# Graph layers on one core: the order of folds and first messages around a convolution

## The chip, the cores and the metric

The program runs on one core of one Trainium2 chip. The metric is the device time of one execution in microseconds (us), lower is better. TensorE multiplies matrices into PSUM, VectorE (DVE), ScalarE (ACT) and GpSimd (POOL) work elementwise, SyncE (SP) issues most transfers.

## The reference

Four graph layers follow each other on a tensor x of 8 batches, 2048 nodes and 64 features, each with a layer norm, a relu and a residual. The change lies in the second one (layer 1), a Chebyshev convolution with weights of its own for each node, and at the border to the third (layer 2), which takes three steps of messages over the same adjacency matrix:

```python
def _L1_gnn_ref(x, A, embedding, weight, bias):
    w = jnp.einsum('nd,dkio->nkio', embedding, weight)
    b = jnp.einsum('nd,do->no', embedding, bias)
    As = [jnp.eye(N, dtype=x.dtype), A, 2.0 * (A @ A) - I]
    x_g = jnp.einsum('knm,bmc->bnkc', jnp.stack(As, 0), x)
    return jnp.einsum('bnki,nkio->bno', x_g, w) + b
...
for _ in range(MAX_STEPS):        # layer 2, v = normed x
    effects = jnp.einsum('nm,bmd->bnd', adj_matrix, v)
    h = jax.nn.relu(jnp.einsum('bnk,dk->bnd', concat([v, effects]), W1) + b1)
    v = jnp.einsum('bnk,dk->bnd', h, W2) + b2
```

(The second listing is shortened; As stands for what the loop of the reference builds with K = 3.)

## The kernel before

Features lie on partitions, two batches in one tile of 128, so the 8 batches are four pairs (q = 0 to 3). The 2048 nodes are worked on in four chunks of 512 columns.

The stage concerned is the second half of `chebyshev_layer` (from L1338). `adj_product` (L302) forms adj times adj h for one chunk at a time. Its 16 steps m each load 128x512 of adj transposed (L313, five buffers), cast it on ACT into one of two buffers (L325), and issue eight matmuls of 512 columns: four with the high halves and four with the low halves of the stationary operand, into the PSUM banks pp0 to pp3. After each step it calls `after`, here `some` (L1359), which takes one piece of work off the list `waiting`. At the chunk's end it calls `done2` (L1364).

`done2` first empties the list. Then it loads 2 MB of node embeddings in two halves (emb, L1377) and the chunk of x (L1387), copies the product out of PSUM (L1389), and runs the convolution: for each pair q four blocks, each of four results `pk` of two products each (sixteen matmuls in the trace), which DVE multiplies by emb (L1416) and GpSimd then adds into two sums `acc` (L1421), four additions of a block, two in the first one. When a pair is done, a *fold* is put at the head of the list: `fold_up` (L1353) multiplies the two sums by `fold` into the bank `po` and adds the result to x (L1357). During the pair that follows, `some` takes it off at the block with `blk == 2`. The fold of the last pair stays on the list, and behind it come two pieces: `first` (L1430: the store of x and the first half of the next layer norm, with means by `center`, squares, sums by `to_rows`, root and reciprocal L273) and the second half (scale rows by `from_rows`, and the products into v, L1348). In the first three chunks these three are taken off after steps 0, 1 and 2 of the next chunk's product.

In the fourth chunk the list starts with twelve *first messages* (`first_messages`, one for each 128 nodes of the finished chunks): four small products of 128 columns, eight matmuls in the trace, from v into a bank `pk`, then a high half on ACT (L232) and a low half on DVE (L233). Here `some` is called at every block. Three of the 16 calls take a fold, twelve a message and the last finds nothing; the fold of the last pair, `first`, the second half and the four messages of the last chunk then follow in this order (L1437 to L1441) before layer 2. Layer 2 starts with a small matmul of `aa` and `wt`, and then its own `adj_product`.

The banks `pk` of the convolution, the messages and the norm rotate over three buffers of one name. Each engine works its instructions off in the order in which the build lays them down; a scheduler decides it, largely in the order of the source, and may take a ready piece ahead, as one `center` matmul before the last fold.

Of the kernel before, what the change touches and what calls it, by code (L numbers as in the profile page):

```python
# [27 lines left out]
NC = N // CW  # L28
# [99 lines left out]
class Kernel:  # L128
# [1144 lines left out]
    def chebyshev_layer(self, slots, k):  # L1273
# [29 lines left out]
        fold = k.tile([P, D], F, name="fold")  # L1303
# [34 lines left out]
        with (  # L1338
            tc.tile_pool(reuse_waits="tile", name="conv", bufs=2) as w,
            tc.tile_pool(reuse_waits="tile", name="conv_ps", bufs=1, space=PSUM) as ps,  # L1340
        ):
            steps, u_n = self.steps, self.source
            emb_dram = a["embT"]
            v = Halves(slots, "v", ("q0", "q1"), False)
            waiting = []

            def write(q, ch, xr, scale):
                nc.vector.tensor_mul(v(q)[:, ch * CW : (ch + 1) * CW], xr, scale)  # L1348

            def bank():  # L1350
                return ps.tile([P, CW], F, name="bank", tag="pk", bufs=3)

            def fold_up(x, q, accs):  # L1353
                po = ps.tile([P, CW], F, name="po")
                for i, h in enumerate((lo, hi)):
                    self.mm(po[h], fold, accs[i])
                nc.vector.tensor_add(x[:, q], po, x[:, q])  # L1357

            def some(*_):  # L1359

                if waiting:
                    waiting.pop(0)()

            def done2(ch, out):  # L1364
                while waiting:
                    some()
                if ch == 0:
                    steps.prepare(bank)
                if ch == NC - 1:
                    for t in range(NT - TC):  # L1370
                        waiting.append(
                            lambda t=t: steps.first_messages(v, u_n, t, bank())
                        )
                s = slice(ch * CW, (ch + 1) * CW)
                emb = slots.tile([P, NBLK, CW], F, name="emb", tag="q4")
                for j in range(2):
                    nc.sync.dma_start(  # L1377
                        emb[j * D : (j + 1) * D],
                        bass.AP(
                            tensor=emb_dram.tensor,  # L1380
                            offset=emb_dram.offset + j * N + ch * CW,
                            ap=[[0, D], [2 * N, NBLK], [1, CW]],
                        ),
                    )
                two = slots.tile([P, 2, NP, CW], F, name="two", tag="q5")
                aah, x = two[:, 0], two[:, 1]
                nc.sync.dma_start(x, self.xs[1][ch])  # L1387
                for q in range(NP):
                    nc.scalar.copy(aah[:, q], out[q])  # L1389
                free = 0  # L1390
                for q in range(NP):
                    accs = [w.tile([P, CW], F, name="acc", bufs=4) for _ in range(2)]
                    sides = list(enumerate(((xe, lo), (xo, hi))))
                    for blk in range(0, NBLK, 2):
                        pks = {}
                        for b in (blk, blk + 1):
                            for half, (src, h) in sides:

                                tag = ("pk", "pp0", "pp1", "pk", "pp2", "pp3", "pk")[free % 7]
                                free += 1  # L1400
                                pk = ps.tile(
                                    [P, CW], F, name="pk", tag=tag, bufs=3 if tag == "pk" else 1
                                )
                                pks[b, half] = pk
                                c = slice(b * P, (b + 1) * P)
                                self.mm(pk, w01[half][:, c], src(q)[:, s], stop=False)

                        for b in (blk, blk + 1):
                            for half, (src, h) in sides:
                                c = slice(b * P, (b + 1) * P)  # L1410
                                self.mm(pks[b, half], w2[h, c], aah[h, q], start=False)
                        for b in (blk, blk + 1):
                            for half in range(2):
                                acc = accs[half]
                                y = acc if b == 0 else w.tile([P, CW], F, name="y", bufs=3)
                                nc.vector.scalar_tensor_tensor(  # L1416
                                    y, pks[b, half], bias[:, b : b + 1], emb[:, b],
                                    op0=OP.add, op1=OP.mult,
                                )
                                if b > 0:  # L1420
                                    nc.gpsimd.tensor_add(acc, acc, y)  # L1421
                        if blk == 2:
                            some()
                        elif ch == NC - 1:
                            some()
                    waiting.insert(0, lambda q=q, accs=accs: fold_up(x, q, accs))
                std = w.tile([P, CW], F, name="std", tag="y", bufs=3)
                norm = self.norm_parts(ch, x, emb[:, :NP], aah, std, bank, write)

                def first():  # L1430
                    self.store_x(1, ch, x)
                    next(norm)

                waiting.extend((first, lambda: next(norm, None)))

            self.adj_product(ah_n, w, ps, done2, after=some, bufs=5, step=1, casts=2)
            while waiting:  # L1437
                some()

            for t in range(NT - TC, NT):  # L1440
                steps.first_messages(v, u_n, t, bank())  # L1441
# [922 lines left out]
```

## Time and profile before

| | us |
|---|---|
| median of three runs | 2153.69 |
| lowest and highest | 2149.0, 2154.99 |
| the profiled execution | 2148.51 |
| its span | 2146.8 |

Busy time over the span: PE (TensorE matmul) 1914.5 us (89%), DVE 1134.1 (53%), ACT 714.7 (33%), POOL 702.4 (33%). The four chunks of layer 1's convolution stage take the stretch from about 807 to 1350 us. A view of waits names the instruction that waited, the instruction that released it, the total, the number and the longest. A timeline shows start, length, engine, line, operation and tiles, the number of merged instructions, and in brackets the idle time before them and what ended it. A table of stretches gives for each engine the busy time and the number of instructions, then the share of TensorE's clock that was granted (1.00 is full), the share of the 16 DMA engines and what they moved.

### The profile page before, as it was taken

To read this page: it belongs to the slowest core of one execution; us is meant where nothing else is said; L and a number is where in the kernel's file an instruction comes from. 1 tells how busy PE (TensorE), PEld (TensorE's weight loads), DVE (VectorE), ACT (ScalarE), POOL (GpSimd) and SP (SyncE) were. 2 spreads that over 40 slices of the span, in tenths; PEclk is the share of its full clock that TensorE was granted. 3 is DMA by queue.
4 is the path that set the end of the run, shared out by engine and by line. 5 is a ranking of instruction groups with operands and counts; after the bars stand their busy time and mean duration, and the time that the engine had idled before them with its cause. 6 is when DMAs were issued, how large, how long until landed. Compare 5 with 4: busy or idle time off the path is not lost. (4 is left out here: it accounts for less than half of the span.)

```text
span 2146.8 us, 21291 instructions
## 1 busy us (share of the span) xinstructions
PE 1914.5 (89%) x7461; PEld 1153.1 (54%) x7466; DVE 1134.1 (53%) x1932; ACT 714.7 (33%) x1351; POOL 702.4 (33%) x595
## 2 busy tenths in 40 slices
PE   5868999977779999999999998999999999679875
PEld 1425766642237774353443543677777666345432
DVE  7877677737660224424334255698603222249774
ACT  6412555535543440020100201335335333258400
POOL 0000466765300006617357065001000000177770
PEclk8868999988869999999999999999999999879997
DMA  8230333441034360140320401456533443475665
GB/s 320 82 110 4 102 104 118 133 171 43 36 94 134 119 177 14 32 125 0 102 56 5 118 1 60 138 186 235 166 118 125 151 145 131 158 210 162 180 181 180
DMA packets 108797, 253.66 MB, mean 118 GB/s; under 512 B 20912, under 2 KB 21056, under 8 KB 101376
## 3 DMA queue, kind: packets, MB, share of 16 engines
q1 hardware_dynamic: 89264, 181.45, 26.7%
q0 software_dynamic: 17104, 66.47, 10.0%
q10 hardware_dynamic: 2304, 4.20, 0.5%
q8 instruction: 63, 1.03, 0.2%
q14 instruction: 62, 0.51, 0.1%
HBM read 218.30 MB, written 33.78 MB: 117 GB/s over the span
## 5 line engine op out<-in xcount | busy, mean ns | idle before, releaser
L325 ACT CAST adj<-adj_t 128x512 fp32r<-128x512 f32 x384 | 237.3, 619 | 685.9 <-PE pp L166 349.5
L1421 POOL TENSOR_TENSOR acc<-acc,y 128x512 f32<-128x512 f32 x224 | 277.1, 1268 | 444.9 <-DVE y L1416 444.9
L166 PE MATMUL pp<-adj,hi 128*128 128x512 f32 x1280 | 364.4, 404 | 4.4 <-ACT adj L325 4.2
L166 PE MATMUL pk<-q,w 128*128 128x512 f32 (+1 forms) x1024 | 356.5, 609 | 1.8 <-ACT q L1389 1.6
L166 PE MATMUL pp<-adj,lo 128*128 128x512 f32 x1280 | 356.3, 398 | 0.0
L166 PEld LDWEIGHTS pp<-adj,hi 128*128 128x128 f32 x1280 | 241.2, 190 | 77.0 <-issue 16.2
L166 PEld LDWEIGHTS pp<-adj,lo 128*128 128x128 f32 x1280 | 242.7, 190 | 55.6
L166 PEld LDWEIGHTS pk<-q,w 128*128 128x128 f32 (+1 forms) x1024 | 136.2, 188 | 210.2 <-issue 165.9
L1416 DVE SCALAR_TENSOR_TENSOR y<-pk,bias,q 128x512 f32<-128x512 f32 x224 | 157.7, 745 | 142.7 <-PE pk L166 133.2
L166 PE MATMUL acc<-q,ident 128*128 128x512 f32 x416 | 203.4, 615 | 28.4 <-DVE q L2151 16.4
L2061 POOL DMA_INDIRECT ring<-f_rows,near x121 | 140.3, 1160 | 67.5 <-issue 30.2
L166 PEld LDWEIGHTS acc<-q,ident 128*128 128x128 f32 x416 | 76.7, 195 | 104.7 <-issue 47.7
L2165 POOL IOTA q<- 128x2048 int32 x1 | 1.8, 1834 | 316.6 <-PE p L166 316.6
L166 PE MATMUL pp<-adj,x_ind_hi 128*128 128x512 f32 x256 | 94.7, 487 | 2.1 <-DVE q L751 1.9
L166 PE MATMUL bank<-std,from_rows 32*128 32x512 f32 x128 | 45.5, 858 | 54.4 <-DVE std L273 34.5
L1853 POOL TENSOR_TENSOR q<-q,beta 128x512 f32<-128x512 f32 x57 | 67.9, 1192 | 54.6 <-DVE beta L1829 30.8
L1416 DVE SCALAR_TENSOR_TENSOR acc<-pk,bias,q 128x512 f32<-128x512 f32 x32 | 22.6, 746 | 118.1 <-PE pk L166 118.1
L2132 DVE TENSOR_TENSOR q<-ring,e 128x1024 f32<-128x1024 f32 x58 | 70.0, 1218 | 9.3 <-PE acc L166 9.1
L273 DVE RECIPROCAL std<-std 128x512 f32<-128x512 f32 x16 | 53.6, 3351 | 36.7 <-ACT std L272 36.6
L166 PE MATMUL pp<-adj,x_ind_lo 128*128 128x512 f32 x256 | 71.7, 399 | 0.0
L1543 POOL DMA_INDIRECT q<-in_adj_dram,order x15 | 17.2, 1146 | 160.3 <-DVE top L1557 134.0
L166 PEld LDWEIGHTS pp<-adj,x_ind_hi 128*128 128x128 f32 x256 | 48.5, 190 | 38.7 <-issue 23.7
(410 smaller groups left out, 2695.8 us busy)
## 6 DMA issues: line engine op xcount, KB each, us to landing
adj_t<-in_adjT_dram SPq DMA_DIRECT2D x128, 512.0 KB, 3.9
adj_t<-in_adjT_dram SPq DMA_DIRECT2D x128, 256.0 KB, 3.3
rows<-in_adj_dram SPq DMA_DIRECT2D x16, 1024.0 KB, 6.0
q<-x SPq DMA_DIRECT2D x10, 1024.0 KB, 4.8
x<-q SPq DMA_DIRECT2D x9, 1024.0 KB, 4.0
q<-in_embT_dram SPq DMA_DIRECT2D x8, 1024.0 KB, 12.1
x_ch<-in_xT_dram SPq DMA_DIRECT2D x4, 1024.0 KB, 6.0
h_rows<-q SPq DMA_DIRECT2D x16, 256.0 KB, 3.6
```

What stands on the lines that cost most here:

```text
L166: self.nc.tensor.matmul(out, lhsT, rhs, start=start, stop=stop)
L273: nc.vector.reciprocal(std, std)
L325: nc.scalar.copy(moving, at[:, i])
L1416: nc.vector.scalar_tensor_tensor(y, pks[b, half], bias[:, b : b + 1], emb[:, b], op0=OP.add, op1=OP.mult,)
L1421: nc.gpsimd.tensor_add(acc, acc, y)
L1543: nc.gpsimd.indirect_dma_start(row, None, self.a["adj"], bass.IndirectOffsetOnAxis(ap=order[:, 1, t : t + 1], axis=0),)
L1853: self.nc.gpsimd.tensor_tensor(x, x, by.unsqueeze(2).to_broadcast([P, NB, D]), op=OP.mult)
L2061: self.nc.gpsimd.indirect_dma_start(to, None, self.kern.f_rows[:], bass.IndirectOffsetOnAxis(ap=index, axis=0))
L2132: nc.vector.tensor_tensor(y.rearrange("n i (b f) -> n i b f", b=NB), block[:, i : i + 2, : NB * D].rearrange("n i (b f) -> n i b f", b=NB) ...
L2165: nc.gpsimd.iota(whole, pattern=[[1, N]], base=0, channel_multiplier=0)
```

## The change

In the first three chunks an empty piece of work is put at the head of the list, so that step 0 of the next product is followed by nothing, step 1 by the fold, step 2 by `first` and step 3 by the second half. In the fourth chunk `some` is called only while more than five pieces are on the list, so that five messages (those of node tiles 7 to 11) are left; after the chunk these five, the last fold and the two halves of the norm are put into one hand-written order.

```diff
+            LEFT = 5
...
-                        if blk == 2:
-                            some()
-                        elif ch == NC - 1:
+                        if len(waiting) > LEFT if ch == NC - 1 else blk == 2:
                             some()
...
-                waiting.extend((first, lambda: next(norm, None)))
+                rest = first, lambda: next(norm, None)
+                if ch < NC - 1:
+
+                    waiting.insert(0, lambda: None)
+                    waiting.extend(rest)
+                else:
+                    fold, *left = waiting
+                    assert len(left) == LEFT
+                    waiting[:] = left[0], fold, left[1], rest[0], *left[2:], rest[1]
```

What a message is:

```python
pn = bank.rearrange("n (q f) -> n q f", q=NP)
for q in range(NP):
    self.kern.mm(pn[:, q], v(q)[:, t * P : (t + 1) * P], self.w1e)
self.kern.split(u_n, t, bank)
```

As built, the fourth chunk's end reads on TensorE: last convolution block, message 7, fold, message 8, four means, sums, messages 9 to 11, scale rows, messages 12 to 15. The line numbers of the changed kernel are one higher from L1344 on and seven higher behind this function.

## The prediction

> **What bounds the kernel now.** I read the table of stretches first, then TensorE's waits between 870 and 1345 us (the convolution stage of layer 1), then the timelines at the places where those waits lie. Stretches; the columns are length, busy time and instructions of PE, PEld, DVE, ACT, POOL, then TensorE's clock, DMA share and GB/s:
>
> ```profile
> 946.00:1037.90 91.90, 91.90 (x270) 34.47 (x268) 44.02 (x64) 2.88 (x6) 64.29 (x52) 1.00 0.02 7
> 1219.90:1322.70 102.80, 102.61 (x365) 45.19 (x363) 51.74 (x79) 8.59 (x16) 64.68 (x54) 1.00 0.00 1
> ```
>
> These are the convolutions of the second and the fourth chunk. TensorE is busy throughout, so what is moved about inside costs its own TensorE time and no more: the fourth holds twelve first messages, and (102.80-91.90)/12 = 0.91 us is the price of one. GpSimd is free a third of the time. So time is lost only where TensorE waits:
>
> ```profile
> PE po L166 <- POOL acc L1421: 8.2, 4, 2.8
> PE bank L166 <- DVE std L273: 4.2, 1, 4.2
> PE pp L166 <- ACT adj L325: 4.2, 3, 2.4
> PE pk L166 <- ACT q L1389: 1.6, 1, 1.6
> ```
>
> Some 20 us in all. The 8.2 us are four waits of the last fold of a chunk; the first three look alike:
>
> ```profile
> 899.40 1.27 PE L166 MATMUL pp<-adj,hi 128*128 128x512 f32 x4
> 900.51 1.09 PE L166 MATMUL pp<-adj,lo 128*128 128x512 f32 x4
> 903.40 2.29 PE L166 MATMUL po<-acc,fold 128*64 128x512 f32 x4 [1.80 <-POOL acc L1421]
> 905.63 1.19 PE L166 MATMUL pp<-adj,hi 128*128 128x512 f32 x4
> ```
>
> The first step of adj's product ends at about 901.6; the fold waits until 903.40 for GpSimd's last sums, and the second step stands behind it. The wait of 1.6 us, after the third chunk's product, is ACT's:
>
> ```profile
> 1083.62 0.62 ACT L325 CAST adj<-adj_t 128x512 fp32r<-128x512 f32 x1 [4.29 <-DMA adj_t<-in_adjT_dram]
> 1084.15 2.04 ACT L1389 COPY q<-pp 128x512 f32<-128x512 f32 x4
> ```
>
> ACT's queue holds the next chunk's first cast ahead of the four copies that the convolution needs, and that cast waits for a load that stands behind 1 MB of emb. Last, the end of the fourth chunk, and the clock (column after POOL) in it:
>
> ```profile
> 1322.76 1.13 PE L166 MATMUL bank<-q,center 128*128 128x512 f32 x2
> 1326.67 2.29 PE L166 MATMUL po<-acc,fold 128*64 128x512 f32 x4 [2.78 <-POOL acc L1421]
> 1328.89 2.84 PE L166 MATMUL bank<-q,center 128*128 128x512 f32 x6
> 1331.66 1.86 PE L166 MATMUL bank<-q,to_rows 128*32 128x512 f32 x8
> 1337.75 2.08 PE L166 MATMUL bank<-std,from_rows 32*128 32x512 f32 x6 [4.22 <-DVE std L273]
> 1342.60 5.36 PE L166 MATMUL bank<-w1e,q 128*128 128x128 f32 x32
> 1349.47 0.38 PE L166 MATMUL bank<-aa,wt 64*128 64x2 f32 x2 [1.51 <-DVE lo L233]
> ```
>
> ```profile
> 1323.00:1327.00 4.00, 1.22 (x3) 0.25 (x3) 2.42 (x4) 0.60 (x1) 4.00 (x4) 1.00 0.00 0
> 1338.00:1341.00 3.00, 2.23 (x7) 0.66 (x8) 1.89 (x8) 0.00 (x0) 0.00 (x0) 0.50 0.75 289
> 1344.00:1347.00 3.00, 3.00 (x21) 3.00 (x20) 1.82 (x9) 1.17 (x2) 0.29 (x1) 0.69 0.00 0
> ```
>
> From the last convolution matmul (1322.76) to layer 2's first (1349.47) are 26.7 us with little work: it waits for GpSimd, for the reciprocal, and then runs at half clock.
>
> **What the Trainium skill says.** "TensorE: Matmul & The Clock Gate", Part 1, What's actually happening: after about 3.4 us without work the TensorE clock halves, and about 3.4 us of work restore it. The trace agrees: after the wait of 2.78 us the clock stays 1.00, after the 4.22 us it is 0.50. "DMA: Bandwidth & Descriptors", Queues, rings and completion order: what one issuing queue puts on a DMA engine is consumed in order. That fits adj loads stuck behind emb: an emb half issued at 921.62, an adj load at 922.50, and the cast that needs it begins at 934.50.
>
> **The change part by part.** Counts of instructions on all engines stay; only their order changes (GpSimd's not at all).
>
> *1. Three chunk changes.* Built, the order becomes step 0, step 1, fold, step 2, mean and variance, then two steps and three matmuls more before the scale rows: everything of the old chunk comes one step later against adj. A step takes 1.83 us (lo matmuls start at 1198.85 and 1200.69). Step 1 can run at once: its cast, like step 0's, is done during the convolution (ACT is idle for 93 us before the cast of step 2 at 901.68). It ends at 903.4, just when the fold begins today; step 2 then stands where step 1 stood (905.63). Gain 1.80 each, 3 x 1.80 = 5.4 us; bounds 4.5 and 5.5. What it moves on SP: store of x, load of x and both halves of emb, each one adj load later (the second half of emb in the same place before the next chunk's loads). They keep their clock time, while TensorE and the adj loads are one step on; so adj's step 12 instead of 11 is caught behind emb, for the same wait (now 2.4, 0.3 and 1.5 us). I price this at 0, bounds -2 and +6 in all. Emb has slack: a first product with it starts about 5 us after the convolution begins, and the loads queued between the halves become four instead of five. At the end, the store of x and layer 2's first adj loads (issued from 1332.06, first cast at 1347.59) keep their place behind the last fold's addition.
>
> *2. ACT's queue.* In the built order the next chunk's first cast moves behind the four copies, in both places where it stood ahead. The 1.62 us go; as this wait appeared in one of two places and hangs on a load's landing, bounds 0 and 1.6. I take 1.6, for its own execution.
>
> *3. Five messages out of the fourth chunk.* 5 x 0.91 = 4.5 us earlier at the last convolution matmul. Cover: TensorE is full without them (second chunk). GpSimd's four sums take 4.94 us of a block that shrinks from 6.45 us (messages start at 1289.98 and 1296.43) to 5.55 (weight loads at 891.93 and 897.48 in the second last block of the first chunk), so it still keeps up; the third fold stands one block (5.55 us) after its sums' last input, which need 5.2, so no wait, at most 0.3. The last block's own slow start (about 0.4 us, a PSUM bank in the messages' rotation) goes too; I leave it as a margin.
>
> *4. The end.* Let T be the end of the last fold: 6.1 us after the last convolution matmul, set by GpSimd (5.1) and a fold half; it stays, message 7 filling the idle time. Before: layer 2's gate (aa,wt) comes at T+20.6. After, message 8 (0.95) stands before the means, and the first of the four means (0.95) was run ahead of the fold before, now not. Means, rows and reciprocal take 9.5 us from the first mean to the reciprocal's end (907.58 to 917.08 in the second chunk), so it ends at T+10.45 against T+8.8. Messages 9 to 11 run during it, but their low halves (DVE, 0.68 each) stand behind the reciprocal and ahead of the four scale products, and hold the banks: first product at T+12.6 instead of T+11.0, the last ends near T+15.9 instead of T+15.1 (cold matmuls and 1.2 us of small DVE work lie between the first two today, half of that later). TensorE's longest idle time becomes some 2.2 us, so the clock should stay full: messages 12 to 15 save about 1 us of 5.4. But ACT has two adj casts (0.62 each), not one, ahead of the last high half. Sum: the gate at T+20.4 to T+21.5; I take T+21.3, a loss of 0.7. Bounds -0.2 and +3 (a cold clock again, at half speed for some 3 us).
>
> *Sum.* 5.4+1.6+4.5-0.7 = 10.8 us. TensorE stays the bound through layer 2 (198.7 of 200 us busy from 1400 on), so it is carried to the end. The profiled execution took 2148.5 (span 2146.8), so 2137.7; the median of the three runs, 2153.7, lies 5.2 higher, which gives 2142.9. Near the median, leaning a little to the profiled one: **2142 us**. A measurement of this kernel tells about 0.3% (6.5 us) from no change.
>
> **Rivals.**
> - *Only the folds pay.* The tail takes back what part 3 gives (low halves ahead of the scale products, a cold clock), and ACT's wait turns up elsewhere. For it: the four products wait for DVE today too. Against: it needs +3.8 in part 4. 5.4 off, 2148: no difference.
> - *All of it and more.* The clock stays full and the bank's slow start goes: 5.4+1.6+5.0+1.5 = 13.5, 2139.
> - *Slower: emb crowds out adj.* Emb's second half comes one adj load earlier in a queue already at 232 GB/s and 0.98 share (932 to 936 us). If it shares the engines with the adj loads ahead of it instead of following them, 1 MB at 232 GB/s, 4.5 us, falls into each of three chunks: 13.6 against 10.8, 2157. It decides from 3.6 us a chunk. Against: emb's second half is already out (930.2) before three late adj loads land today, and they come 2.0 us apart.
> - *The change does nothing*: excluded, the built order differs as described.
>
> **How the numbers follow.** Forecast 0.60, more 0.15, folds only 0.18, slower 0.07. Range 2134 to 2151: below, the larger gain set from the lower runs; above, folds only with the spread of the runs (2149 to 2155). Faster by over 0.3%: 0.75 of the first two less 0.04 for the spread, and 0.05 of folds only, which lies just inside the bound: 0.76. Within 0.3%: 0.04 and the other 0.13: 0.17. Slower 0.07.
>
> **What would show it.** Right: TensorE's wait for GpSimd's sums at three folds under 0.5 us and each product stretch 1.8 us shorter; no wait for L1390's copies (L1389 before); the fourth convolution some 98 us; clock 1.00 between the reciprocal and layer 2; gate 26 to 28 us after the last convolution matmul. Wrong: longer waits of casts on adj_t, a third fold that waits, a gate beyond 30 us.

## The result, and the profile after

| | us |
|---|---|
| before, median of 15 runs | 2150.42 (2146.24 to 2158.15) |
| changed, median of 15 runs | 2138.89 (2135.89 to 2146.53) |
| ratio, 95% interval | 0.9949, 0.9936 to 0.9962 |
| profiled execution, before and changed | 2148.51 and 2138.25 |

The changed kernel is faster by about 11 us (8.2 to 13.8). The forecast was 2142 with a sum of 10.8 us, so the total is met. Its parts are not. The table cuts both profiled executions at the same places on TensorE; differences are changed minus before.

| stretch | before | changed | difference | predicted |
|---|---|---|---|---|
| up to the first convolution | 806.71 | 808.36 | +1.65 | 0 |
| first convolution | 92.69 | 92.69 | 0.00 | 0 |
| three products of adj, chunks 2 to 4 | 135.02 | 124.66 | -10.36 | -5.4 |
| second and third convolution | 185.47 | 183.39 | -2.08 | -1.6 |
| fourth convolution | 102.87 | 97.95 | -4.92 | -4.5 |
| from its end to layer 2's gate (aa,wt) | 26.71 | 29.27 | +2.56 | +0.7 |
| from the gate to layer 2's first adj matmul | 3.45 | 5.14 | +1.69 | 0 |
| the rest | 793.88 | 795.04 | +1.16 | 0 |

The first and the last row hold nothing that the change touches; in the profiles of this study the first lies between 806.4 and 809.3 us, whichever kernel ran. The last one holds, in the profile of the changed kernel and not in that of before, an interval at half clock in layer 2 (1381.44 to 1384.86), which costs some 1.7 us by estimate (half of 3.41). The chunk changes brought twice what was predicted. The end gave back nearly all that the fourth convolution gained.

TensorE's waits between 870 and 1345 us in the changed kernel (who waited, for whom; total, times, longest):

```profile
PE bank L166 <- DVE lo L233: 3.8, 2, 1.9
PE po L166 <- POOL acc L1422: 3.2, 4, 2.8
PE bank L166 <- DVE q L1349: 2.3, 3, 0.8
PE pp L166 <- ACT adj L325: 2.2, 2, 1.7
```

Of the 8.2 us for GpSimd's sums 3.2 are left, nearly all of it at the last fold of the stage. The wait for the copies is gone, that for the casts is halved. At a chunk change the timeline of TensorE now reads:

```profile
901.05 1.27 PE L166 MATMUL pp<-adj,hi 128*128 128x512 f32 x4
902.17 1.09 PE L166 MATMUL pp<-adj,lo 128*128 128x512 f32 x4
903.09 1.08 PE L166 MATMUL pp<-adj,hi 128*128 128x512 f32 x4
904.01 1.08 PE L166 MATMUL pp<-adj,lo 128*128 128x512 f32 x4
905.12 2.29 PE L166 MATMUL po<-acc,fold 128*64 128x512 f32 x4
```

Two steps run before the fold, and no wait stands ahead of it. Its length will matter below. The windows of the first of these products, of the second and of the fourth convolution (length; busy time of PE, PEld, DVE, ACT, POOL; TensorE's clock, DMA share, GB/s):

```profile
901.05:942.41 41.36, 39.95 (x159) 26.51 (x158) 10.65 (x16) 13.11 (x23) 5.02 (x4) 1.00 0.64 169
942.41:1034.10 91.69, 91.69 (x269) 34.50 (x267) 44.38 (x65) 2.61 (x6) 64.35 (x52) 1.00 0.05 16
1209.10:1307.05 97.95, 97.95 (x326) 40.76 (x324) 48.81 (x74) 5.66 (x11) 64.71 (x54) 1.00 0.00 1
```

The end of the fourth chunk, TensorE's timeline:

```profile
1307.05 1.16 PE L166 MATMUL bank<-w1e,q 128*128 128x128 f32 x8
1310.96 1.07 PE L166 MATMUL po<-acc,fold 128*64 128x512 f32 x2 [2.75 <-POOL acc L1422]
1312.18 1.07 PE L166 MATMUL po<-acc,fold 128*64 128x512 f32 x2 [0.15 <-POOL acc L1422]
1313.18 1.16 PE L166 MATMUL bank<-w1e,q 128*128 128x128 f32 x8
1314.18 3.62 PE L166 MATMUL bank<-q,center 128*128 128x512 f32 x8
1317.73 1.86 PE L166 MATMUL bank<-q,to_rows 128*32 128x512 f32 x8
1319.52 2.94 PE L166 MATMUL bank<-w1e,q 128*128 128x128 f32 x24
1324.37 3.45 PE L166 MATMUL bank<-std,from_rows 32*128 32x512 f32 x8 [1.90 <-DVE lo L233]
1327.75 6.64 PE L166 MATMUL bank<-w1e,q 128*128 128x128 f32 x32
1336.32 0.38 PE L166 MATMUL bank<-aa,wt 64*128 64x2 f32 x2 [1.93 <-DVE lo L233]
1336.63 5.40 PE L166 MATMUL pp<-q,w1v 128*128 128x512 f32 x8
```

The same view's windows give the clock behind the scale rows and behind the gate:

```profile
1322.40:1324.40 2.00, 0.10 (x2) 0.04 (x1) 2.00 (x3) 0.59 (x1) 0.00 (x0) 1.00 0.98 376
1327.70:1331.00 3.30, 3.30 (x16) 3.25 (x16) 2.29 (x22) 0.28 (x1) 0.00 (x0) 0.50 0.00 0
1336.30:1341.40 5.10, 5.08 (x9) 2.30 (x10) 1.92 (x6) 0.12 (x1) 0.00 (x0) 0.67 0.61 200
```

The order is the one that was foreseen, and no idle time is longer than 2.75 us. Still messages 12 to 15 run at half clock: 32 matmuls of the trace in 6.64 us, where 24 of them at full clock took 2.94 us just before. Layer 2's first eight matmuls take 5.40 us; before they took 3.70.

### The profile page after: what moved, and what is told of

Its sections match the earlier page's. It is cut to its first block, busy times and chain, and to the rows that moved or that the text cites. A ratio compares the mean times of both kernels' runs of the same rounds, so it can differ in the third digit from the quotient of the medians.

```text
span 2136.5 us, 21290 instructions
## 1 busy us (share of the span) xinstructions
PE 1914.3 (90%) x7461; PEld 1153.6 (54%) x7466; DVE 1128.8 (53%) x1932; ACT 715.0 (33%) x1351; POOL 704.7 (33%) x595
## 3 DMA queue, kind: packets, MB, share of 16 engines
q0 software_dynamic: 17104, 66.47, 10.1%
## 5 line engine op out<-in xcount | busy, mean ns | idle before, releaser
L166 PEld LDWEIGHTS pp<-adj,hi 128*128 128x128 f32 x1280 | 240.8, 190 | 74.3 <-issue 15.9
```

Source lines behind the costliest of these rows:

```text
L166: self.nc.tensor.matmul(out, lhsT, rhs, start=start, stop=stop)
```

## The experiments

Eleven kernels. The diffs are against the changed kernel. The table gives what the profiles show: the three products together, the fourth convolution, and the stretch from its start to layer 2's first adj matmul, which holds all that part 3 and part 4 of the prediction are about; then the timed ratio to the kernel before. All durations in us.

| run | products | 4th conv. | its start to layer 2 | ratio, 95% interval |
|---|---|---|---|---|
| before | 135.02 | 102.87 | 133.03 | |
| changed | 124.66 | 97.95 | 132.36 | 0.9949, 0.9936 to 0.9962 |
| e1_chunks_only | 123.96 | 102.87 | 132.48 | 0.9923, 0.9894 to 0.9952 |
| e2_fourth_only | 131.25 | 97.95 | 132.55 | 0.9991, 0.9978 to 1.0003 |
| e3_three_three | 123.69 | 97.06 | 128.90 | 0.9918, 0.9897 to 0.9938 |
| e4_filled | 123.52 | 97.95 | 130.38 | 0.9918, 0.9898 to 0.9937 |
| e5_two_empty | 118.87 | 97.95 | 130.93 | 0.9931, 0.9909 to 0.9954 |
| e6_after_again | 123.24 | 97.94 | 133.94 | 0.9937, 0.9916 to 0.9958 |
| e7_four_three | 124.20 | 96.16 | 129.93 | 0.9933, 0.9916 to 0.9950 |
| e8_two_ahead | 123.33 | 97.95 | 133.89 | one run |
| e9_two_four_three | 123.41 | 96.16 | 126.64 | 0.9888, 0.9870 to 0.9906 |
| e10_four_bufs | 127.79 | 97.95 | 136.25 | 0.9968, 0.9947 to 0.9990 |
| e11_two_chunks_only | 118.87 | 102.87 | 137.70 | 0.9931, 0.9910 to 0.9952 |

(In e10 the build puts two matmuls of each convolution, 0.87 us, ahead of the product's last steps; they are counted with the convolution here.)

**Each half alone.** e1_chunks_only leaves the fourth chunk as it was:

```diff
-                        if len(waiting) > LEFT if ch == NC - 1 else blk == 2:
+                        if ch == NC - 1 or blk == 2:
...
-                    waiting[:] = left[0], fold, left[1], rest[0], *left[2:], rest[1]
+                    waiting.extend(rest)
```

> Only the three empty pieces are put in; the fourth chunk is as before the change. Theory (the parts add up: folds 5.4, ACT's queue 1.6): about 7 us below before, 0.9967; TensorE's wait for the sums at the first three folds under 0.6 us in all, no wait for the copies of the product; the fourth chunk's convolution 102.9 us and its end 26.7 us as before. Rival (the messages carry the gain): less than 3 us.

e2_fourth_only leaves the chunk changes as they were:

```diff
-                    waiting.insert(0, lambda: None)
```

> Only the fourth chunk's part; the first three changes of chunk as before. Theory after the result's trace (4.9 us out of the convolution, 2.6 us back at the chunk's end, 1.7 us at layer 2's first matmuls with half a clock): 0.5 to 1.5 us below before, 0.9994, not told apart from no change. The prediction's own sum (4.5 less 0.7): 3.8 us below, 0.9982. Rival (the messages carry the gain): 7 us or more below.

The first alone is worth 0.9923, 16.6 us (10.3 to 22.8), against 7.0 in the prediction's parts 1 and 2. The second alone is worth 0.9991, 1.9 us off, between 4.7 off and 0.6 more. So the gain is the chunk changes'. e2's waits, with the old order at the chunk changes:

```profile
PE po L166 <- POOL acc L1422: 8.3, 5, 2.8
PE pk L166 <- ACT q L1390: 3.3, 2, 1.7
PE pp L166 <- ACT adj L325: 2.9, 3, 1.6
```

Here the wait for the copies behind the caught cast comes at two of the three chunk changes, where the kernel before had it at one. Its second and third convolution together take 187.24 us, against 183.4 in every kernel with the new order: part 2 is worth 3.8 us here and 2.1 in the profile of before.

**Where the products got shorter.** The windows of the first two products in the kernel before are 46.62 us with 41.50 busy and 44.23 with 41.25 busy; the timeline of the second shows why the busy time differs from the 39.9 of the third:

```profile
1042.27 3.19 PE L166 MATMUL po<-acc,fold 128*64 128x512 f32 x4 [1.80 <-POOL acc L1421]
...
1072.84 1.21 PE L166 MATMUL pp<-adj,hi 128*128 128x512 f32 x4 [0.26 <-ACT adj L325]
```

The window of the 3.3 us from this fold on, columns as above, with the clock third from the right:

```profile
1042.20:1045.50 3.30, 3.23 (x5) 0.68 (x5) 0.00 (x1) 0.00 (x0) 1.24 (x2) 0.51 0.24 78
```

After a wait of only 1.80 us the fold and what followed ran at half clock. In the first product it came after the cast's wait of 2.41 us (clock 0.57 from 936 to 940). So the 10.36 us are: waits of folds 5.41 to 0.30, that is 5.1; waits for casts 4.18 to 2.21, 2.0; half clock, 41.50 to 39.95 and 41.25 to 39.74 busy, 3.1; together 10.2. In e2's three products, with the same waits of folds, the clock stayed at 1.00, so the third item isn't there in every execution: 131.25 us against 135.02.

**A second empty piece** of work, so that three steps run ahead of the fold:

```diff
-                    waiting.insert(0, lambda: None)
+                    waiting[:0] = [lambda: None, lambda: None]
```

> The change with two empty pieces instead of one in the first three chunks. Theory (the gain there is the fold's wait of 1.8 us, which is gone already, and what hangs on TensorE being ahead of the norm's loads): the three products stay at 40.6 to 42.6 us each and the time at the changed kernel's, 0.993 to 0.995. Rival (the waits of casts behind the emb loads shrink with each step that TensorE is ahead): another 0.4 to 0.8 us a product less. Other rival (emb comes too late for the convolution, one step less remaining): first products with emb wait, products or convolutions longer by 1 us or more.

The fold in TensorE's timeline of this kernel:

```profile
905.15 1.08 PE L166 MATMUL po<-acc,fold 128*64 128x512 f32 x4
```

And the window of the first product, columns as above:

```profile
899.35:938.98 39.63, 38.78 (x159) 26.32 (x158) 10.64 (x16) 13.12 (x23) 5.06 (x4) 1.00 0.63 170
```

The products take 39.6 us each, and in none does TensorE wait for a fold or a cast. The fold itself falls from 2.29 to 1.08: with one step ahead, its second half still waited for the second sum (in the changed kernel GpSimd's last addition ends at 906.28, 1.16 us after the fold began), inside what the timeline shows as one group (where the trace does split such a fold, at 1310.96 and 1312.18 above, each half shows 1.07 us and only 0.15 count as idle). The rest are the casts' waits of the changed kernel, 0.47 and 1.74 us in two of the three products. So the theory on record, products as in the changed kernel, fails in this profile. It is not that TensorE reaches the late load later: it comes to the step caught behind emb 11.14 us after emb's first half is issued in the first product and 11.6 in the third, as in the changed kernel. The load landed sooner, 10.1 to 10.8 us after that issue against 10.6 to 12.6. As timed (0.9931, four runs) this can't be told from the changed kernel; its profiled execution, at 2128.99, is the fastest of its four.

**One buffer less for adj's loads:**

```diff
-            self.adj_product(ah_n, w, ps, done2, after=some, bufs=5, step=1, casts=2)
+            self.adj_product(ah_n, w, ps, done2, after=some, bufs=4, step=1, casts=2)
```

> The changed kernel with four instead of five buffers for the loads of adj in this product. Theory (what the step moved ahead bought beyond the fold's wait is lead: the load caught behind emb is waited for less because TensorE is further from needing it): with one buffer less each load is issued one step (1.8 us) later and the wait for a cast is back, some 1 to 2 us in each of the three chunk changes; product stretches 42.3 to 43.3 us instead of 41.3, no wait of the fold for GpSimd, about +3 to +6 us on the changed kernel, ratio to the kernel before 0.997 to 0.999. Rival (the landing after emb has its own time, independent of when the load was issued): product stretches 41.3 as before, ratio 0.994.

The products take 42.55, 42.40 and 42.83 us, 1.2 to 1.8 more than those of e6 (the changed kernel once more), and the ratio is 0.9968 (0.9947 to 0.9990, which overlaps the changed kernel's). In the first two products the wait for the cast is back. In the first, the timeline of ACT:

```profile
934.53 1.29 ACT L325 CAST adj<-adj_t 128x512 fp32r<-128x512 f32 x2 [4.82 <-DMA adj_t<-in_adjT_dram]
```

and that of TensorE, which waits for this cast:

```profile
935.20 1.20 PE L166 MATMUL pp<-adj,hi 128*128 128x512 f32 x4 [1.66 <-ACT adj L325]
```

The first half of emb is issued at 923.36 and the load caught behind it is ready at 934.53, 11.2 us later; with five buffers (emb at 923.35) TensorE waits at this place for 0.47 us, until 934.96. The caught load is issued 0.89 us behind emb in both kernels and lands at about the same time (934.43, and 934.19 with five buffers). With four it is the load of one step earlier, and TensorE comes to it 10.18 us after emb's issue instead of 11.14: a step of 1.83 us less, and 0.87 us of convolution matmuls more. So what decides here is how many steps TensorE still has in hand when the load lands. The second product waits for 1.17 us. In the third the wait is only 0.38 us; there an interval at half clock (1190.58 to 1193.99) makes up most of the difference.

**The end of the fourth chunk.** Is it the idle time that lowers the clock? e4_filled puts two dense products (four matmuls in the trace, into the fold's bank, a result that nobody reads) behind message 11:

```diff
+            def fill():
+                po = ps.tile([P, CW], F, name="po")
+                for i in range(2):
+                    self.mm(po, ident, xe(0)[:, :CW], start=i == 0, stop=i == 1)
...
-                    waiting[:] = left[0], fold, left[1], rest[0], *left[2:], rest[1]
+                    waiting[:] = left[0], fold, left[1], rest[0], *left[2:], fill, rest[1]
```

> The change with two matmuls more, 512 columns of identity times data into the fold's own bank, whose result nobody reads, in the 2 us in which TensorE waits ahead of the scale rows. Theory (half a clock after that wait costs 1 us in the scale rows and messages and 1.7 us at layer 2's start): the clock stays near 1.00 to the gate, the gate comes 1 to 2 us earlier after the fold, 2 to 3 us below the changed kernel, 0.9937. Rival (low halves and ACT's casts set the end, the clock hardly matters): same as the changed kernel within 1 us.

TensorE's timeline from the two products to message 15:

```profile
1322.24 1.88 PE L166 MATMUL po<-q,ident 128*128 128x512 f32 x4
1324.29 3.18 PE L166 MATMUL bank<-std,from_rows 32*128 32x512 f32 x8 [0.18 <-DVE lo L233]
1327.40 5.49 PE L166 MATMUL bank<-w1e,q 128*128 128x128 f32 x32
```

The windows of the scale rows and of what follows:

```profile
1323.90:1326.90 3.00, 2.82 (x9) 1.17 (x8) 2.98 (x9) 0.00 (x0) 0.00 (x0) 1.00 0.11 41
1326.90:1329.90 3.00, 3.00 (x12) 2.50 (x12) 2.94 (x24) 0.00 (x0) 0.00 (x0) 0.52 0.00 0
```

The idle time is down to 0.18 us, TensorE is busy throughout, and the clock falls to 0.52 all the same, a little later and for less long. What runs there is the scale rows, matmuls over 32 rows. So idle time alone doesn't explain the loss, and filling it doesn't cure it; the end of this section comes back to the scale rows.

**Messages ahead of the fold.** In the changed kernel one of them fills the wait for GpSimd, and 2.75 us stay idle. e8 puts two there, of five; e3 three, of six; e7 four, of seven:

```diff
-                    waiting[:] = left[0], fold, left[1], rest[0], *left[2:], rest[1]
+                    waiting[:] = *left[:2], fold, rest[0], *left[2:], rest[1]
```

```diff
-            LEFT = 5
+            LEFT = 6
...
-                    waiting[:] = left[0], fold, left[1], rest[0], *left[2:], rest[1]
+                    waiting[:] = *left[:3], fold, rest[0], *left[3:], rest[1]
```

```diff
-            LEFT = 5
+            LEFT = 7
...
-                    waiting[:] = left[0], fold, left[1], rest[0], *left[2:], rest[1]
+                    waiting[:] = *left[:4], fold, rest[0], *left[4:], rest[1]
```

> The change with message 8 moved ahead of the last fold, five held as in the change. Theory (message 8 between fold and means lengthens the chain to the reciprocal by its own 0.95 us): from the fold's end to the reciprocal's end 0.9 to 1.0 us less than the changed kernel's 10.5 us; convolution 98.0 us as there. Rival (that chain is set by the addition of x on DVE, and the message is hidden): no difference.

> The change with six messages held, three ahead of the last fold and three behind the means, none between the fold and the means. Theory (what stands between the fold and the reciprocal lengthens the end, what stands ahead of the fold is hidden): reciprocal ends 0.95 us earlier after the fold and the convolution 0.9 us earlier, so 1.9 us below the changed kernel, 0.9940 against before. Rival (GpSimd's sums or the banks hold the fold back when three messages stand ahead of it): same as the changed kernel or slower.

> Seven messages held, four ahead of the last fold, three behind the means. Theory (a message ahead of the fold is hidden until the wait for GpSimd's sums is full): convolution 0.9 us shorter than with six (96.2 us), fold late by 0 to 0.5 us; 0.9914, 0.5 to 0.9 us below the version with six. Rival (the fourth message waits for a bank, whose low half comes behind the last products on DVE): end 1 us or more longer, no gain over six.

With four ahead no idle time stands before the fold (its 1.99 us, against 1.08, still hold a wait of its second half), and the means start 6.16 us after the convolution's end, 6.15 with three: the fourth message is free. From the convolution's start to layer 2 these take 128.90 and 129.93 us, 2 to 4 less than the changed kernel; by the times, 0.9918 and 0.9933, that isn't told apart. e8, with two, has the fold at half clock after 1.40 us of idle time and gains nothing (133.89). Its theory holds in kind: from the fold's end to the reciprocal's end it takes 9.86 us, with the means partly at half clock, and e3 and e7 take 9.61 and 9.62, against 10.51 in the changed kernel. The message between the fold and the means costs its 0.9 us there.

**The changed kernel once more**, to see how much of the end is chance:

> The changed kernel once more, beside the versions of this call. All theories: 0.9949 as before, 0.9936 to 0.9962; convolution of the fourth chunk 98.0 us, its end 29.3 us, layer 2's first chunk with 1.7 us at half clock if the clock falls again.

Its products and convolutions repeat within 0.1 us but for the third product (41.24 against 42.61, a late load). At the end its fold waits 3.44 us and runs at half clock, 3.19 us; the end to the gate takes 30.86 us instead of 29.27.

**Two empty pieces, fourth chunk as before**, the test of the five messages at the shorter products:

```diff
-                        if len(waiting) > LEFT if ch == NC - 1 else blk == 2:
+                        if ch == NC - 1 or blk == 2:
...
-                    waiting.insert(0, lambda: None)
+                    waiting[:0] = [lambda: None, lambda: None]
...
-                    waiting[:] = left[0], fold, left[1], rest[0], *left[2:], rest[1]
+                    waiting.extend(rest)
```

> Two steps of the next product ahead of each of the first three chunks' last folds; the fourth chunk as in the kernel before, all twelve messages in it. Theory (the five messages held back are worth nothing, the end takes back what the fourth convolution gives): fourth convolution 102.9, from its start to layer 2's first adj matmul 131 to 133.5 us, and the whole within 1.5 us of the kernel with two steps ahead and five messages held back, ratio 0.992 to 0.993. Rival (they are worth their 4.9 us less the 0.7 expected at the end): this kernel is 4 us slower than that one, ratio 0.995.

The ratio is 0.9931 like e5's. But its end isn't the one expected: 137.70 us, 5 longer than in e1, whose end is the same code. From TensorE's timeline:

```profile
1309.54 3.19 PE L166 MATMUL po<-acc,fold 128*64 128x512 f32 x4 [2.77 <-POOL acc L1422]
1312.66 4.20 PE L166 MATMUL bank<-q,center 128*128 128x512 f32 x6
...
1327.72 6.09 PE L166 MATMUL bank<-w1e,q 128*128 128x128 f32 x32
```

The fold waited 2.77 us here, 2.78 in the kernel before. There the clock stayed full (2.29 for the fold, 2.84 for the same six means); here it halved. A single profile of the end is thus uncertain by some 5 us, and what the five held messages are worth rests on the times: no gain shown in three comparisons (e2 with before, the changed kernel with e1, e5 with e11), each uncertain by 3 to 7 us.

**The two gains together**, two empty pieces and four messages ahead of the fold of seven:

```diff
-            LEFT = 5
+            LEFT = 7
...
-                    waiting.insert(0, lambda: None)
+                    waiting[:0] = [lambda: None, lambda: None]
...
-                    waiting[:] = left[0], fold, left[1], rest[0], *left[2:], rest[1]
+                    waiting[:] = *left[:4], fold, rest[0], *left[4:], rest[1]
```

> Two steps of the next product ahead of each chunk's last fold, and in the fourth chunk seven messages held back, four of them ahead of the fold, three behind the first half of the norm. Theory (the two gains are independent): each product stretch 39.6 us as with two steps ahead alone (41.3 in the changed kernel: -5.1 us over three), fourth convolution 96.2 (-1.8), end no longer than with four ahead alone (28.7); so about 6 us below the changed kernel, ratio to the kernel before 0.989 to 0.991, some 2128 us. Rival (the end's clock takes back whatever the fourth convolution gains): the stretch from the start of the fourth convolution to layer 2's first adj matmul stays at 131 to 133 us, and the ratio at 0.992 to 0.993, as with two steps ahead alone.

It is the fastest of all: 2128.44 us, ratio 0.9888 (0.9870 to 0.9906), below the changed kernel's interval. Its profile doesn't give the account that was expected. The first product takes 39.29 us, the second 41.24, with some 1.7 us (half of 3.41) lost to half clock where nothing waited for long, the third 42.88, with half clock again and a wait of 1.58 us for a cast (its load landed 14.0 us after emb's first half was issued). From the fourth convolution's start to layer 2 it is the shortest seen; TensorE's timeline of the end:

```profile
1302.22 1.16 PE L166 MATMUL bank<-w1e,q 128*128 128x128 f32 x8
1303.59 2.94 PE L166 MATMUL bank<-w1e,q 128*128 128x128 f32 x24 [0.21 <-DVE y L1417]
1306.46 1.98 PE L166 MATMUL po<-acc,fold 128*64 128x512 f32 x4
1308.37 3.72 PE L166 MATMUL bank<-q,center 128*128 128x512 f32 x8
...
1318.65 3.02 PE L166 MATMUL bank<-std,from_rows 32*128 32x512 f32 x8 [1.89 <-DVE lo L233]
1321.61 5.47 PE L166 MATMUL bank<-w1e,q 128*128 128x128 f32 x32
```

The fold follows the four messages without idle time, and the half clock comes late and is short (messages 12 to 15 in 5.47 us). The profiled execution, at 2132.67, is the slowest of its five timed ones, so part of the gain lies in executions that left no trace; where it lies there stays open. The times say one thing more. e9 differs from e11 in the fourth chunk alone, and their intervals don't meet (0.9870 to 0.9906 and 0.9910 to 0.9952). So messages held back can pay when four of seven stand ahead of the fold, though e7, the same fourth chunk with one empty piece, shows no such gain on e1 (0.9933 and 0.9923).

**Where the clock halves.** The clock of the 13 profiles (the two kernels and the eleven runs) shows one pattern between 880 and 1420 us. It has 42 stretches at half clock. Each lasts 3.41, 6.83 or 10.24 us, and within a profile they all begin on one grid of 3.41 us, which lies differently in each profile. Cut on that grid, the wait of 2.78 us ahead of the fold in the kernel before (first two lines) and the one of 2.77 us in e11 (last two) read, columns as above:

```profile
1321.94:1325.35 3.41, 1.95 (x8) 0.36 (x4) 3.22 (x5) 0.60 (x1) 2.45 (x3) 1.00 0.00 0
1325.35:1328.77 3.42, 1.96 (x4) 0.38 (x4) 0.20 (x1) 0.00 (x0) 2.63 (x4) 1.00 0.00 0
1305.18:1308.60 3.42, 1.58 (x6) 0.30 (x2) 3.12 (x5) 0.60 (x1) 2.82 (x3) 1.00 0.00 0
1308.60:1312.01 3.41, 2.47 (x4) 0.58 (x4) 0.00 (x0) 0.00 (x0) 2.25 (x3) 0.50 0.00 0
```

In the kernel before the wait is shared between two intervals with 1.95 and 1.96 us of work (PE's busy time) each, and the clock stays full. In e11 more of it falls into one, which has 1.58 us, and the next interval runs at half clock. Of the intervals at full clock without scale rows, all 17 with up to 1.45 us of work have half clock behind them and none with more than 1.90 us has; in between both occur. Scale rows count for less than their time, although no run changes them alone. In e9's second product:

```profile
1048.77:1052.19 3.42, 2.65 (x12) 0.70 (x10) 1.93 (x4) 0.52 (x1) 0.00 (x0) 1.00 0.44 145
1052.19:1055.60 3.41, 3.41 (x9) 2.73 (x9) 0.74 (x2) 0.62 (x1) 0.00 (x0) 0.50 0.29 54
```

Of these 2.65 us of work 2.22 are scale rows. There are 22 such intervals with 2.64 or 2.65 us of work. The four in which the other matmuls have up to 0.61 us are followed by half clock; the 18 in which they have 0.78 us or more are not. In e4 the interval ahead of the half clock has 3.23 us of work, 2.75 of it scale rows; in the changed kernel (1323.42 to 1326.83) it has 2.46, all of it scale rows.

## Why the prediction was right in its total, point by point

- **Part 1, the folds' waits** (5.4 us): right. They fell by 5.1, and in e2, where only this order is undone, they are back.
- **Part 1, the loads behind emb** ("for the same wait", "I price this at 0, bounds -2 and +6"): wrong in size. The waits for casts fell by 2.0 in the profiled pair, at the good edge of the bounds. The reckoning that TensorE and the load keep their places to each other holds: TensorE comes to the caught step 11.14 us after emb's first half is issued in the first product, and 11.60 in the third, before and after the change. What it took as fixed was the landing. The caught load landed 11.1 to 12.8 us after that issue in the six products of the old order (before, e2; mean 11.9), 10.4 to 12.6 in the 24 with one empty piece (mean 11.0), and 10.0 to 11.0 in eight of the nine with two, 14.0 in the ninth. The ranges overlap, and why it lands sooner isn't settled.
- **Part 1, what isn't in the sum**: the half clock behind the waits of the old chunk changes, 3.1 us in the profile of before. The windows of the first two products show it, as a clock of 0.96; the prediction read the clock only at the end of the stage. Likewise the fold's 2.29 us were taken for its own length, while the kernel before has a fold of the same four matmuls in 1.08 us (at 1302.87). That 1.2 us of hidden wait is still in the changed kernel, and e5 takes it out.
- **Part 2** (1.6, "bounds 0 and 1.6"): right in kind, too small. The wait could come up at two chunk changes, not one, and does in e2. It never comes up in a kernel with the new order.
- **Part 3** (4.5, with 0.4 left as a margin): right, and the margin came too: 4.92, the same in seven profiles with five messages held.
- **Part 4** ("the clock should stay full", gate at T+21.3, a loss of 0.7): this is the step that failed. The order, the reciprocal (T+10.5) and the scale products (the last ends at T+15.3, 15.9 reckoned) are as worked out, but messages 12 to 15 run at half clock, 6.64 us instead of some 4.4, and the gate comes at T+23.1. The longest idle time is 2.75 us and not 2.2, since message 7 took the place of the mean that ran ahead of the fold before; but that one left the clock full. What precedes the half clock is the interval that holds nothing but scale rows (2.46 us of them in 3.41). The half clock reaches on into layer 2's first matmuls, 1.7 us more, which the prediction didn't count. The bound of +3 named this case. The Trainium skill, "TensorE: Matmul & The Clock Gate", Part 1, What's actually happening, was read for its 3.4 us of idle time alone. It also says that the window in which activity is watched runs freely and that the outcome changes from run to run. Here that second sentence agrees with the trace better: the same wait of 2.77 to 2.78 us left the clock full in two profiles (before, e1) and halved it in a third (e11), and the half clocks lie on a grid of 3.41 us. With 3.4 us as a threshold on the longest idle time, e4's loss of clock after 0.18 us can't be explained, nor the half clock behind waits of 1.80 and 2.41 us in the profile of before, which the prediction passed over when it found the page borne out; the measurement decides.
- **The rivals.** "Only the folds pay" had the end right, nothing left of part 3, and the total wrong, since it had no more than 5.4 for the chunks. "All of it and more" hits the measured total with its 2139, but for a reason that didn't hold, a clock that stays full. "emb crowds out adj" is refuted: the waits for casts became shorter. The total of 10.8 came out because parts 1 and 2 were some 5.4 us too small and part 4 some 3.6 us too good, while the first and the last row of the table, which the change doesn't touch, took 2.8 more. So the parts were off by about half of the total, and that they cancelled is luck.

## What to carry to other kernels

Where an engine waits, add to the wait what follows it: TensorE's clock behind it, and the waiting that hides in the length of the group itself; compare that length with the same group at a place where nothing is late. Work that is put ahead of a late result can move the later loads along with it: here the distance from emb's issue to the step that waits behind it stayed at 11.14 and 11.60 us, and the waits shrank because the load landed sooner. So count the steps in hand at each later wait, and measure the landing by itself. Work held back for a stretch with gaps shows no gain if the clock falls in that stretch; look at the clock's windows there before a gain is booked. Whether one wait costs the clock depends on where it falls on the clock's grid, so don't judge it by a single profile.

## What was not expected of the hardware

- TensorE's clock fell to half after waits of 1.4 us (e8) and 1.8 us (before, second chunk), and to 0.52 with no idle time above 0.18 us, behind matmuls over 32 rows (e4); after 2.75 to 2.78 us it stayed full in before, in the changed kernel, e1 and e2, and halved in e4, e5 and e11. Over all 13 profiles it halves for whole intervals of 3.41 us on a grid, behind an interval with little work by TensorE (1.45 us or less always, more than 1.90 never, scale rows apart).
- The scale rows, matmuls over 32 rows, keep the clock up less than their time suggests: with 2.65 us of work in an interval it halved when other matmuls had 0.61 us or less of it, and stayed when they had 0.78 or more.
- Two halves of a fold into 64 columns each take 1.08 us for all four matmuls when both sums are there, and 1.07 us for each half when they come apart (e5 and the changed kernel): one after the other they cost double.
